# Four-layer cross-attention stack on one Trainium2 core: block transposes of L1's self layers moved behind the next unit's maxima, their DMAs on two queues, V's bias on TensorE, sums of x on ScalarE

## The chip, the core and the metric

The kernel runs on one core of one Trainium2 chip. A core has five engines with queues of their own: TensorE (PE in the profile; PEld is its weight load), VectorE (DVE), ScalarE (ACT), GpSimd (POOL) and SyncE (SP), which here only issues DMAs. All DMAs of the core are carried out by its 16 DMA engines. The metric is the device time of one execution in microseconds.

## The reference

Four layers follow one another on x (4 batches, 1024 tokens, 256 channels) and a context of 77 tokens. L0 is self attention with a mask, cross attention and a feed-forward; L2 and L3 are cross attentions with 16 heads. The change touches L1, which applies its layer three times: the first time to the context, then twice to itself (`enc` attends to `enc`). Cut to what matters:

```python
def _mha_layer(q, k, v, Wq, bq, Wk, bk, Wv, bv, gamma, beta):   # H = 4 heads of 64
    Q = relu(q @ Wq + bq);  K = relu(k @ Wk + bk);  V = relu(v @ Wv + bv)
    scores = einsum('hbqd,hbkd->hbqk', Qh, Kh) / sqrt(64)
    key_mask = sign(abs(sum(k, axis=-1)))
    scores = where(key_mask[None, :, None, :] == 0.0, NEG, scores)
    attn = softmax(scores)
    query_mask = sign(abs(sum(q, axis=-1)))
    attn = attn * query_mask[None, :, :, None]
    out = einsum('hbqk,hbkd->hbqd', attn, Vh) ... + q
    return layer_norm(out, gamma, beta)

q, k, v = queries, keys, values
for i in range(3):
    enc = _mha_layer(q, k, v, Wq[i], bq[i], Wk[i], bk[i], Wv[i], bv[i], gamma[i], beta[i])
    enc = leaky_relu(enc @ Wff[i] + bff[i], negative_slope=0.2) + enc
    q, k, v = enc, enc, enc
```

Everything is computed in fp32. The sum of x over its channels, which gives the two masks, is one of the things that move.

## The kernel before

x stays on the chip, one tile of 128 partitions x 8 x 256 for each batch. The program is a list of items, one for each layer and batch: `Cross16` (L0's cross attention, L2, L3), `Cross4` (L1's first layer, on the context) and `Self4` (L1's layers 1 and 2 on themselves). `Pipe.run` takes them one after the other. An item's attention is cut into units. For `Self4` a unit is a pair of heads p (0 or 1) and a tile t of 128 queries (0 to 7), so an item has 16 units; `Pipe.unit` does one:

1. what was put off as "full" to this unit,
2. `scores(p, t)` (L1206): eight matmul passes into two PSUM tiles `ss`, one for each head (L1213); for each head the maximum over 1024 keys on VectorE, negated (L1224), and the exponential with its sum on ScalarE into `PR` (L1230),
3. what was put off as "next",
4. the pump, which fills in steps of the next item's start (turning x, V, Q and K) and of the last item's end (normalizing, the layer with `Wff`), by their costs,
5. what was put off as "turn", "late" and "col".

`pipe.later(kind, delay, f)` puts a piece of work off to a unit that lies `delay` ahead. The order of TensorE's instructions is the order in which the program writes them. On the other engines the planner of the tile framework sets the order, with buffers and dependencies as it sees them; each engine then runs its queue strictly in order.

The products with V need the exponentials with keys on the partitions. In the branch that the inputs take (`net.blocks`), this is done in blocks of 32: VectorE transposes each 32 x 32 block of `PR` in place (`turned_by_blocks`, L1242), and for each pair of units 16 DMAs of 128 KB (L1249) carry block row a to partition group c of the tile `PT`. All 16 go out on SP's queue. `weighted` (L1285) then multiplies `PT` with V in two halves of eight keys blocks' worth of matmuls, `normal` (L1303 to L1315) turns the result back, divides by the sums and adds x. There are two `PR` buffers, each for a pair of units, two `PT` buffers, and four small PSUM tiles (`p1`) for everything beside the scores.

Three other places matter. `Self4.start` computes the sum of x over channels (L1103) on VectorE, and from it the factor `f` of the query mask and the row `neg` of the key mask; `masks` (L1127) turns `neg` into a row. `values` (L1142) makes V for two tiles of tokens: eight matmul passes, an add of the bias row `brow`, spread over the partitions by a POOL DMA (L1145), and a relu times `f` on ScalarE (L1147). `Layer4.load` fetches a layer's weights and rows; `Net.thirds` (L1992) splits an fp32 row into three bf16 rows, so that a matmul with a row of ones (`ones_rowb`) can add it in PSUM; the layer with `Wff` does that for its bias already (L1353).

Of the kernel before, what the change touches and what calls it, by code (L numbers as in the profile page):

```python
# [9 lines left out]
F32 = mybir.dt.float32  # L10
# [7 lines left out]
P = 128  # L18
# [958 lines left out]
class Layer4:  # L977
# [6 lines left out]
    def load(self):  # L984
# [26 lines left out]
        rows = net.tile("OT", [1, C], name="rows")  # L1011
        nc.sync.dma_start(out=rows, in_=t["rows"][ROW[name] : ROW[name] + 1, C : 2 * C])
        self.rows = net.thirds(rows, C)
        self.brow = net.wpool.tile([P, C], F32, tag="row", name="row", bufs=2)
        nc.gpsimd.dma_start(out=self.brow, in_=t["rows"][ROW[name], 0:C].partition_broadcast(P))
# [67 lines left out]
class Self4(Item):  # L1083
# [4 lines left out]
    def start(self):  # L1088
# [5 lines left out]
        def new():  # L1094
            self.hT = net.tile("C", [P, NC, S], name="hT")
            if l.n:
                self.later_half = False
                self.v = net.tile("D", [P, NT, C], name="V")
            self.nm = net.small.tile([P, NT, 4], F32, tag="nm", name="nm", bufs=2)
            self.sums = net.small.tile([P, NT, 4], F32, tag="sums", name="sums", bufs=2)  # L1100

            sx = net.small.tile([P, NT], F32, tag="sx", name="sx", bufs=2)
            nc.vector.tensor_reduce(sx, x, AX.X, ALU.add)  # L1103
            self.f = net.small.tile([P, NT], F32, tag="f", name="f", bufs=2)
            nc.vector.tensor_scalar(self.f, sx, 0.0, None, ALU.not_equal)
            if l.n:
                self.neg = net.small.tile([P, NT], F32, tag="neg", name="neg", bufs=2)
                nc.vector.tensor_scalar(self.neg, sx, 0.0, MASKED, ALU.is_equal, ALU.mult)
            else:
                self.qt = net.tile("A", [P, 2, S], name="QT")  # L1110
                self.v, self.less = l.v[:, b, :], l.less[:, b : b + 1]
                self.ka = net.work.tile([P, 2, 2, SC], F32, tag="KA", name="KA4", bufs=2)
                nc.gpsimd.memset(self.ka, 0.0)
                for h in range(2):
                    rows = slice(64 * h, 64 * h + 64)
                    nc.gpsimd.tensor_copy(self.ka[rows, :, h, :], l.kt[rows, :, ts(b, SC)])

# [6 lines left out]
        def masks():  # L1124

            pm = net.p1.tile([P, 512], F32, tag="p1", name="pm")
# [11 lines left out]
        def values(t):  # L1138
            pv = net.p1.tile([P, 2, C], F32, tag="p1", name="pv")
            for i in range(2):  # L1140
                for cc in range(NC):
                    nc.tensor.matmul(  # L1142
                        pv[:, i, :], self.hT[:, cc, ts(t + i, P)], l.w["wv"][:, cc, :], start=cc == 0, stop=cc == NC - 1
                    )
            nc.vector.tensor_tensor(pv, pv, l.brow.unsqueeze(1).to_broadcast([P, 2, C]), ALU.add)  # L1145
            for i in range(2):
                nc.scalar.activation(self.v[:, t + i, :], pv[:, i, :], AF.Relu, scale=self.f[:, t + i : t + i + 1])  # L1147

        step(0, new)
        for c in range(2):  # L1150
            step(0.5, turn, c, 0)
            step(0.5, turn, c, 1, lag=2 * c)
# [53 lines left out]
    def scores(self, p, t):  # L1206
# [24 lines left out]
        if net.blocks:  # L1231
            net.pipe.later("turn", 0, lambda: self.turned_by_blocks(p, t, self.pr))
# [3 lines left out]
    def turned_by_blocks(self, p, t, pr):  # L1236
# [10 lines left out]
        for c in range(4):  # L1247
            for a in range(4):
                nc.sync.dma_start(  # L1249
# [4 lines left out]
        for half in range(2):  # L1254
            net.pipe.later("next", 3 + half, lambda half=half: self.weighted(p, t, pt, half, state))
# [179 lines left out]
class Net:  # L1435
# [556 lines left out]
    def thirds(self, row, n):  # L1992

        nc = self.nc
        out = self.work.tile([3, n], BF16, tag="thirds", name="thirds", bufs=2)
# [142 lines left out]
```

## Time and profile before

| | us |
|---|---|
| median of 3 runs (lowest, highest) | 2431.14 (2427.19, 2433.52) |
| the profiled execution | 2428.16 |
| its span | 2426.3 |

| share of the span | busy us | instructions |
|---|---|---|
| PE | 2201.2 (91%) | 11003 |
| DVE | 1620.2 (67%) | 3200 |
| ACT | 907.2 (37%) | 1700 |
| POOL | 104.2 (4%) | 142 |

Times are microseconds from the start of the span. A line of a group names the source line, the engine, the operation, the tile written and the tiles read, the shapes and the number of instructions; behind the bar stand busy time and mean nanoseconds of one, and then how long the engine had stood idle just before them and what ended most of that. A busy time is the time in which at least one instruction of the group ran. The ends of matmuls are modelled, so that a busy PE is not a PE at its peak. A line of the waits names who waited for whom, the sum in us, how often, and the longest. A line of the timeline begins with the start and the length in us. Issues of DMAs are not counted as busy time.

The self layers of L1 fill the stretch from 937 us (first maximum) to 1904 us (last block transpose). In the 100 us from 1400 to 1500, for example, PE is busy for 94.25, DVE for 87.96 and ACT for 45.61, and the DMA engines move 149 GB/s.

### The profile page before, as it was taken

Reading aid. Unit: us, or ns where it says so; the run is one execution under the profiler, and the core shown is the slowest. Engines: PE = TensorE matmul, PEld = TensorE weight load, DVE = VectorE, ACT = ScalarE, POOL = GpSimd, SP = SyncE. Lnnn points to the kernel's source line nnn. Section 1 sums busy time; section 2 is a strip of 40 time slices with the busy share of each in tenths; the row PEclk is TensorE's granted clock in tenths of the full one; section 3 lists DMA queues with packets and bytes.
Section 4 is the critical chain, followed back from the end, with each engine's and each line's share of the span. In section 5 each row is a group of like instructions: output and inputs, shape, how many; then the busy total and the mean of one; then the engine's idle time right before and its main releaser. Section 6 shows DMA issues by size and latency. Waiting matters only on the chain. (4 is left out here: it accounts for less than half of the span.)

```text
span 2426.3 us, 29759 instructions
## 1 busy us (share of the span) xinstructions
PE 2201.2 (91%) x11003; PEld 1233.3 (51%) x11003; DVE 1620.2 (67%) x3200; ACT 907.2 (37%) x1700; POOL 104.2 (4%) x142
## 2 busy tenths in 40 slices
PE   4899999999999989999998999999998898899886
PEld 2566546666768655544444544444444444454332
DVE  5566655444243777888888788888888655565665
ACT  1222342222331544444444445444433343334333
POOL 2000000000000000000000000000000000000000
PEclk7999999999989989999999999989999898899888
DMA  4000010000000001766665666666675300000000
GB/s 127 18 1 16 5 35 1 1 7 5 7 5 3 1 5 45 157 150 139 139 144 134 146 148 148 139 139 139 156 160 130 70 5 1 5 1 1 27 18 28
DMA packets 197593, 158.18 MB, mean 65 GB/s; under 512 B 51327, under 2 KB 196030, under 8 KB 197438
## 3 DMA queue, kind: packets, MB, share of 16 engines
q1 hardware_dynamic: 195374, 152.45, 27.3%
q0 software_dynamic: 1008, 2.68, 0.5%
q8 instruction: 90, 1.47, 0.3%
q10 hardware_dynamic: 1056, 1.05, 0.1%
q14 instruction: 65, 0.53, 0.1%
HBM read 17.67 MB, written 4.19 MB: 9 GB/s over the span
## 5 line engine op out<-in xcount | busy, mean ns | idle before, releaser
L1230 ACT ACTIVATE PR<-ss,nm 128x1024 f32<-128x1024 f32 x256 | 284.4, 1113 | 398.9 <-DVE nm L1224 313.1
L1242 DVE STREAM_TRANSPOSE PR<-PR 128x2048 f32<-128x2048 f32 x128 | 295.8, 2311 | 113.4 <-ACT PR L1230 109.9
L1213 PE MATMUL ss<-QK 64*128 64x512 f32 x1024 | 336.9, 650 | 38.1 <-ACT PR L1230 37.8
L1224 DVE TENSOR_REDUCE nm<-ss 128x1 f32<-128x1024 f32 x256 | 299.8, 1210 | 9.5 <-PE ss L1213 9.4
L1285 PE MATMUL po<-PT,V 128*64 128x256 f32 x2048 | 261.3, 399 | 9.0 <-DMA PT<-PR 6.8
L356 ACT ACTIVATE PT<-pb 77x1024 f32<-77x1024 f32 x192 | 185.4, 1016 | 173.7 <-PE pb L352 173.7
L1285 PEld LDWEIGHTS po<-PT,V 128*64 128x64 f32 x2048 | 141.7, 141 | 171.6 <-issue 109.2
L1213 PEld LDWEIGHTS ss<-QK 64*128 64x128 f32 x1024 | 116.7, 193 | 181.9 <-ACT PR L1230 105.7
L275 DVE TENSOR_REDUCE mx<-pa 128x4 f32<-128x308 f32 x384 | 157.6, 469 | 74.2 <-PE pa L270 73.1
L270 PE MATMUL pa<-KA,QT 64*128 64x308 f32 x768 | 170.9, 499 | 33.7 <-DVE mx L275 31.1
L270 PEld LDWEIGHTS pa<-KA,QT 64*128 64x128 f32 x768 | 103.4, 201 | 101.9 <-DVE mx L275 46.8
L365 PE MATMUL po<-PT,Vc 77*32 77x512 f32 x768 | 135.7, 646 | 18.9 <-ACT PT L356 10.2
L1452 ACT COPY OT<-po 128x512 f32<-128x512 f32 x57 | 33.4, 586 | 230.1 <-PE po L365 218.4
L595 PE MATMUL pp<-w,hid 128*128 128x256 f32 x512 | 114.0, 381 | 0.0
L580 PE MATMUL pp<-hF,w 128*128 128x256 f32 x512 | 113.2, 379 | 0.0
L346 PE MATMUL pb<-QT,KA 32*77 32x512 f32 x768 | 112.7, 658 | 0.0
L595 PEld LDWEIGHTS pp<-w,hid 128*128 128x128 f32 x512 | 96.5, 190 | 15.9 <-DVE mx L275 2.5
L580 PEld LDWEIGHTS pp<-hF,w 128*128 128x128 f32 x512 | 97.1, 190 | 14.6 <-issue 1.3
L1483 DVE BATCH_NORM_STATS2 st<-x 128x6 f32<-128x256 f32 x256 | 97.9, 404 | 5.6 <-DMA x<-in_x 4.4
L1356 PE MATMUL pp<-wo,hE 128*128 128x256 f32 x384 | 96.4, 393 | 1.6 <-ACT hE L1459 1.5
L588 ACT ACTIVATE hid<-pp,cols 128x256 f32<-128x256 f32 x64 | 30.4, 474 | 175.7 <-PE pp L580 175.7
L260 PE MATMUL pp<-hT,wq 128*128 128x512 f32 x192 | 91.2, 611 | 1.8 <-DVE hT L1450 1.0
(253 smaller groups left out, 3042.3 us busy)
## 6 DMA issues: line engine op xcount, KB each, us to landing
PT<-PR SPq DMA_DIRECT2D x1024, 128.0 KB
x<-in_x SPq DMA_DIRECT2D x4, 1024.0 KB
out<-x SPq DMA_DIRECT2D x8, 512.0 KB
w<-in_ff_w SPq DMA_DIRECT2D x2, 1024.0 KB
gb<-in_norms POOLq DMA_DIRECT2D x5, 256.0 KB, 4.8
wk<-in_l_wk SPq DMA_DIRECT2D x10, 128.0 KB
wv<-in_l_wv SPq DMA_DIRECT2D x5, 256.0 KB
wq<-in_l_wq SPq DMA_DIRECT2D x10, 128.0 KB
```

The costliest lines, as they stand in the source:

```text
L270: nc.tensor.matmul(pas[i], self.qt[rows, e, ts(t, P)], self.ka[rows, e, :, :], start=True, stop=True)
L275: nc.vector.tensor_reduce(out, pas[i].rearrange("p (j s) k -> p j s k", s=2), AX.X, ALU.max, negate=True)
L346: nc.tensor.matmul(pbs[j // 2][:SC, j % 2, :], self.ka[rows, e, 2 * (j % 2) + s, :], self.qt[rows, e, ts(c, 512)], start=True, stop=False,)
L356: nc.scalar.activation(pt[:, 2 * i : 2 * i + 2, :], pbs[i][:SC], AF.Exp, scale=self.l.scale)
L365: nc.tensor.matmul(po[ts(j, h.slot), :], l.v[:, self.b, col : col + h.vw], pt[:, j, :], start=True, stop=True)
L580: nc.tensor.matmul(pp[:, i, :], self.w1[:, cc, ts(f + i, P)], s["hT"][:, cc, ts(q, 2 * P)], start=cc == 0, stop=cc == NC - 1)
L595: nc.tensor.matmul(pp[:, u, :], s["a"][:, f, ts(u, P)], self.w2[:, f, :], start=f == 0, stop=f == NF - 1)
L1213: nc.tensor.matmul(ss[h][:, k, :], self.qk[p][rows, 0, ts(t, P)], self.qk[p][rows, 1, ts(k, 512)], start=True, stop=True,)
L1224: nc.vector.tensor_reduce(self.nm[:, t, at], s2, AX.X, ALU.max, negate=True)
L1230: nc.scalar.activation(out, s2, AF.Exp, bias=self.nm[:, t, at], accum_out=self.sums[:, t, at])
L1242: nc.vector.transpose(part, part)
L1285: nc.tensor.matmul(po[64 * h : 64 * h + 64], self.v[:, k, 64 * (2 * p + h) : 64 * (2 * p + h) + 64], pts[:, :, h, :, k, :] if net.blocks e ...
```

## The change

- The block transpose of a unit (with the 16 DMAs after each second one) is put off to "next" of the following unit, which is behind that unit's maxima in the program; before it stood at "turn" of its own unit.
- Of the 16 DMAs, those with odd a go out on POOL's queue and those with even a on SP's.
- The products with V are put off to "turn", 2 and 3 units after the transpose's new place; that is the same unit as before, but behind the pump's steps instead of ahead of them.
- The bias of V is added in PSUM by a matmul with a row of ones and the three thirds of the bias (`vrows`), in layers 1 and 2; the add on VectorE and the POOL DMA of the bias row go. `load` makes a second set of thirds, and `thirds` gets four buffers instead of two.
- The sum of x over channels comes from ScalarE in layers 1 and 2: an activation for each tile of tokens that writes a copy nobody reads and accumulates the sum, two of them after each turning step; the masks are made from it in `masks`.

```diff
@@ Layer4.load
-        rows = net.tile("OT", [1, C], name="rows")
-        nc.sync.dma_start(out=rows, in_=t["rows"][ROW[name] : ROW[name] + 1, C : 2 * C])
-        self.rows = net.thirds(rows, C)
-        self.brow = net.wpool.tile([P, C], F32, tag="row", name="row", bufs=2)
-        nc.gpsimd.dma_start(out=self.brow, in_=t["rows"][ROW[name], 0:C].partition_broadcast(P))
+        def thirds(at):
+            rows = net.tile("OT", [1, C], name="rows")
+            nc.sync.dma_start(out=rows, in_=t["rows"][ROW[name] : ROW[name] + 1, at : at + C])
+            return net.thirds(rows, C)
+
+        self.rows = thirds(C)
+        if self.n:
+            self.vrows = thirds(0)
+        else:
+            self.brow = net.wpool.tile([P, C], F32, tag="row", name="row", bufs=2)
+            nc.gpsimd.dma_start(out=self.brow, in_=t["rows"][ROW[name], 0:C].partition_broadcast(P))
@@ Self4.start
-            sx = net.small.tile([P, NT], F32, tag="sx", name="sx", bufs=2)
-            nc.vector.tensor_reduce(sx, x, AX.X, ALU.add)
-            self.f = net.small.tile([P, NT], F32, tag="f", name="f", bufs=2)
-            nc.vector.tensor_scalar(self.f, sx, 0.0, None, ALU.not_equal)
-            if l.n:
-                self.neg = net.small.tile([P, NT], F32, tag="neg", name="neg", bufs=2)
-                nc.vector.tensor_scalar(self.neg, sx, 0.0, MASKED, ALU.is_equal, ALU.mult)
-            else:
+            self.sx = net.small.tile([P, NT], F32, tag="sx", name="sx", bufs=2)
+            if not l.n:
+                nc.vector.tensor_reduce(self.sx, x, AX.X, ALU.add)
+                marks()
...
+        def marks():
...
+        def sums(t):
+            out = net.tile("F", [P, 2, C], name="xs")
+            for i in range(2):
+                nc.scalar.activation(out[:, i, :], x[:, t + i, :], AF.Identity, accum_out=self.sx[:, t + i : t + i + 1])
@@ masks
+            marks()
@@ values
+            nc.tensor.matmul(pv, net.ones_rowb, l.vrows.unsqueeze(1).to_broadcast([3, 2, C]), start=True, stop=False)
...
-            nc.vector.tensor_tensor(pv, pv, l.brow.unsqueeze(1).to_broadcast([P, 2, C]), ALU.add)
@@ the steps of start
         for c in range(2):
-            step(0.5, turn, c, 0)
-            step(0.5, turn, c, 1, lag=2 * c)
+            for cc in range(2):
+                step(0.5, turn, c, cc, lag=2 * c * cc)
+                if l.n:
+                    step(0, sums, 4 * c + 2 * cc)
@@ scores
-            net.pipe.later("turn", 0, lambda: self.turned_by_blocks(p, t, self.pr))
+            net.pipe.later("next", 1, lambda pr=self.pr: self.turned_by_blocks(p, t, pr))
@@ turned_by_blocks
-                nc.sync.dma_start(
+                (nc.sync, nc.gpsimd)[a % 2].dma_start(
...
-            net.pipe.later("next", 3 + half, lambda half=half: self.weighted(p, t, pt, half, state))
+            net.pipe.later("turn", 2 + half, lambda half=half: self.weighted(p, t, pt, half, state))
@@ Net.thirds
-        out = self.work.tile([3, n], BF16, tag="thirds", name="thirds", bufs=2)
+        out = self.work.tile([3, n], BF16, tag="thirds", name="thirds", bufs=4)
```

More of the change, by code (lines that the diff above doesn't have):

```diff
@@ L1116, in new @@
                     nc.gpsimd.tensor_copy(self.ka[rows, :, h, :], l.kt[rows, :, ts(b, SC)])
+        def marks():
+            self.f = net.small.tile([P, NT], F32, tag="f", name="f", bufs=2)
+            nc.vector.tensor_scalar(self.f, self.sx, 0.0, None, ALU.not_equal)
+            if l.n:
+                self.neg = net.small.tile([P, NT], F32, tag="neg", name="neg", bufs=2)
+                nc.vector.tensor_scalar(self.neg, self.sx, 0.0, MASKED, ALU.is_equal, ALU.mult)
+        def sums(t):
+            out = net.tile("F", [P, 2, C], name="xs")
+            for i in range(2):
+                nc.scalar.activation(out[:, i, :], x[:, t + i, :], AF.Identity, accum_out=self.sx[:, t + i : t + i + 1])
         def turn(c, cc):
@@ L1142, in values @@
                     nc.tensor.matmul(
-                        pv[:, i, :], self.hT[:, cc, ts(t + i, P)], l.w["wv"][:, cc, :], start=cc == 0, stop=cc == NC - 1
+                        pv[:, i, :], self.hT[:, cc, ts(t + i, P)], l.w["wv"][:, cc, :], start=False, stop=i + cc == NC
                     )
-            nc.vector.tensor_tensor(pv, pv, l.brow.unsqueeze(1).to_broadcast([P, 2, C]), ALU.add)
             for i in range(2):
@@ L1150, in start @@
         for c in range(2):
-            step(0.5, turn, c, 0)
-            step(0.5, turn, c, 1, lag=2 * c)
+            for cc in range(2):
+                step(0.5, turn, c, cc, lag=2 * c * cc)
+                if l.n:
+                    step(0, sums, 4 * c + 2 * cc)
         if l.n:
```

## The prediction

> **What bounds the kernel now.** I read the page's slices first, to find the stage that the change touches, then its groups, then the waits, the timeline and tables of windows inside that stage, and last the DMA traffic. The slices and groups of the page:
>
> ```profile
> DVE  5566655444243777888888788888888655565665
> ...
> DMA  4000010000000001766665666666675300000000
> ...
> L1230 ACT ACTIVATE PR<-ss,nm 128x1024 f32<-128x1024 f32 x256 | 284.4, 1113 | 398.9 <-DVE nm L1224 313.1
> L1242 DVE STREAM_TRANSPOSE PR<-PR 128x2048 f32<-128x2048 f32 x128 | 295.8, 2311 | 113.4 <-ACT PR L1230 109.9
> ...
> L1224 DVE TENSOR_REDUCE nm<-ss 128x1 f32<-128x1024 f32 x256 | 299.8, 1210 | 9.5 <-PE ss L1213 9.4
> ```
>
> The slices with DMA at 5 to 7 are the two self layers of L1: 128 units (2 layers, 4 batches, 16 units each). They run from 937 to 1904 us, 7.56 us a unit. There ScalarE waits for the maxima (313.1 us), and VectorE's only large wait is that of the block transpose for the exponentials (109.9 us). Units 64 to 79 (batch 0 of layer 2) are a stretch without layer loads; their waits and a table of windows, in which the last columns are granted clock, DMA share and GB/s:
>
> ```profile
> ACT PR L1230 <- DVE nm L1224: 35.6, 11, 4.5
> ...
> DVE PR L1242 <- ACT PR L1230: 14.4, 12, 1.3
> ACT V L1147 <- DVE pv L1145: 12.6, 4, 3.8
> ```
>
> ```profile
> 1416.50:1533.10 116.60, 108.60 (x531) 53.05 (x527) 100.61 (x124) 54.11 (x104) 2.71 (x3) 0.99 0.64 147
> 1200.00:1209.00 9.00, 8.93 (x53) 5.50 (x49) 7.61 (x14) 3.14 (x6) 0.00 (x0) 1.00 0.88 203
> 971.50:973.50 2.00, 2.00 (x18) 1.06 (x16) 2.00 (x3) 0.00 (x0) 0.00 (x0) 1.00 1.01 178
> 973.50:974.50 1.00, 1.00 (x10) 0.86 (x8) 0.97 (x4) 0.12 (x1) 0.00 (x0) 1.00 1.04 320
> 974.50:978.50 4.00, 3.44 (x15) 2.26 (x15) 2.73 (x3) 3.72 (x9) 0.00 (x0) 1.00 1.13 202
> ```
>
> Of 116.6 us VectorE is busy for 100.6; the 16.0 left are nearly all its wait for ScalarE. So VectorE's queue sets the pace: unit time is its work plus that wait. One unit in the timeline:
>
> ```profile
> 1222.01 0.67 DVE L1145 TENSOR_TENSOR pv<-pv,row 128x512 f32<-128x512 f32 x1
> 1222.59 2.34 DVE L1224 TENSOR_REDUCE nm<-ss 128x1 f32<-128x1024 f32 x2
> ...
> 1223.83 1.11 ACT L1230 ACTIVATE PR<-ss,nm 128x1024 f32<-128x1024 f32 x1 [0.28 <-DVE nm L1224]
> ...
> 1224.96 1.11 ACT L1230 ACTIVATE PR<-ss,nm 128x1024 f32<-128x1024 f32 x1
> 1225.08 3.11 PE L1213 MATMUL ss<-QK 64*128 64x512 f32 x8 [0.39 <-ACT PR L1230]
> ...
> 1226.19 2.31 DVE L1242 STREAM_TRANSPOSE PR<-PR 128x2048 f32<-128x2048 f32 x1 [1.27 <-ACT PR L1230]
> ```
>
> Maxima, exponentials, and then VectorE stands 1.27 us until the second exponential is written; only then come the transpose and what is queued behind it.
>
> **The change, part by part.** The five clean batches (1, 2, 4, 5, 6) take 119.4, 118.2, 116.6, 119.9 and 115.3 us from first maximum to first maximum: mean 117.9, or 7.37 a unit. All savings are counted against 7.37; times are against the profiled run (2428.2 us, span 2426.3), which lies 3 below the median 2431.1.
>
> *Transpose behind the next unit's maxima.* The transpose now finds its exponentials long written; the wait (110 us) goes. VectorE's work stays.
>
> *Bias of V on TensorE.* Four adds a batch of 0.68 us leave VectorE (2.7 us), four ones-row matmuls of 0.32 from start to start (the same form at L1353) come to TensorE: 1.3 us. ScalarE's wait for the add (81.5 us in 28) goes too; it was covered.
>
> *Sums of x on ScalarE.* One reduction of 2.28 us a batch leaves VectorE. ScalarE gets 8 activations of at most 0.47 (V's row, 128x256) and 8 accumulator reads of 0.19: 5.3 us a batch on an engine busy 54 of 117. It costs nothing while it does not stand before an exponential; without that cover up to 0.66 for each.
>
> *Floors after these three.* VectorE: 100.6 - 2.7 - 2.3 = 95.6 a batch, 5.97 a unit. TensorE: a unit's scores (1.99) and products with V (1.95) are 63 a batch; 4 V's (1.99), 4 forwards (about 2.3 with the ones row), 8 projections (1.98, half with a ones row) about 35, 48 transposes of 0.11, and 1.3 new: 105 at most; merged rows contain 0.2 of overlapping tail, so about 101, 6.3 a unit, and 6.6 at the stage's granted clock of about 0.95. The loop scores, maximum, exponential, exponential is 2.24 + 0.14 + 1.98 + 1.2 = 5.6. So without the DMAs a unit would take about 6.6.
>
> *What is late next: the block DMAs.* A pair of units (2k, 2k+1) fills one of two PR buffers; 16 DMAs of 128 KB empty it; the first exponential of unit 2k+4 may write it again only when all have landed. So far they start after the transpose in unit 2k+1. Call D the time from the end of that transpose to the last landing. In the trace the 16th issue ends 10.4 to 11.8 us after it, the last packet 11.8 to 13.4, and the exponential comes at 14.6 to 18.5: it was free. Now the transpose of unit 2k+1 comes after the maxima of unit 2k+2, about 1.17 + 2.31 us past the moment at which that unit's first exponential could run, plus 0.4 for what stands between in a few units: 3.9. Follow the loop over four units: exponential of 2k+2, two rounds of the loop (L each) to the maximum of 2k+4, 3.9, then D, then the exponential of 2k+6, which uses the same buffer. So a unit takes the larger of 6.6 and (2L + 3.9 + D)/4. The products with V are due later in unit 2k+4 than before (behind the other matmuls), so they are not the first to wait.
>
> *D with two queues.* SP issues one block DMA each 0.648 us; with eight on SP and eight on POOL, whose issues take 0.53 to 0.60 us, issue ends at about 5 us. Then the transfers set D: first packet 1.3 us after the issue, 2.1 MB at some rate, and 0.35 for the semaphore (landing of POOL's small loads against their last packet). The rate is in the windows above. SP alone moves 203 GB/s with the DMA engines 88% busy. When a POOL load (gb, issued at 970.29) had blocked the blocks, the backlog first ran at 320 GB/s for 1 us, then for 4 us at 202, with the share up to 1.13: more in flight, hardly more moved. In that stretch, by the packet records of the trace, the packets' lag behind their issues fell from 2.58 to 2.00 us over 8 DMAs, which is 0.596 us each, 220 GB/s. Bounds: 178 GB/s (the window in which both queues moved) gives D = 1.65 + 11.8 = 13.4; 320 gives 8.2. I take 215, near the long backlog: D = 1.65 + 9.8 = 11.4.
>
> The Trainium skill (DMA: Bandwidth & Descriptors, section "Issuing engines are not separate DMA queues") says that issuing from several engines saves only the sequencers' issue time, because all run on the same 16 DMA engines. By that rule the rate stays at 203, D is 12.0 and the sum below about 19 us higher; the window at 202 agrees with it, the one at 320 doesn't.
>
> *Sum.* L lies between 5.6 and 6.6; I take 6.4. (12.8 + 3.9 + 11.4)/4 = 7.03 a unit: 0.34 saved x 128 = 43 us.
>
> *POOL's queue.* Each norm's power (L1336, 1.07 us) now shares a queue with the DMAs: behind eight issues it waits 5 us, with two units of slack before its reader in the built order. Bounds 0 to 1 us for each of 16; I take 0.
>
> *Second row of thirds.* Layers 1 and 2 each cast and load one more row: three casts of 0.27, two subtractions of 0.40 and four DMAs on SP between block DMAs. In layer 2 the present load made batch 3 last 127.8, 10 more than the clean mean; one pair's issues stretched to 19.8 us. Bounds 0 and +10; I take +6, as half the blocks now avoid SP. Layer 1's load meets no block DMAs.
>
> Total: -43 + 6 = -37, so 2428.2 - 37 = about 2391 us.
>
> **The rivals.**
> - *The blocks bind nobody.* The two queues drift apart and the drain is nearer 320 GB/s; D is below 9.7 and the unit falls to 6.6: -99 + 6, 2335 us (2320 to 2355). For: the 320 window. Against: it held for 1 us.
> - *No gain.* 203 GB/s and a loop of 6.6: (13.2 + 3.9 + 12.0)/4 = 7.28, -12 + 6: 2422, up to 2435. For: the 202 window.
> - *Slower: two queues in each other's way.* Place: the DMA engines while SP and POOL blocks are both queued. At 178 GB/s D is 13.4 and, with L up to 6.6, the unit 7.63; with POOL's later first packet (1.75 after issue) 7.75: +33 to +49, plus 6 to 10: 2470 to 2485. It decides from D = 12.4 (about 195 GB/s) on. For: the 178 window, where SP's packets nearly stopped. Against: that load read HBM, the blocks don't.
> - *Slower: VectorE holds up POOL's issues.* If each of the eight waits for the end of a VectorE instruction (1.2 us mean), issue takes 9.6 and D is 1.65 + 9.6 + 1.2 = 12.5 at least, and, with more than one instruction each, 14: 2435 to 2490. Against: POOL's loads in this stage went in 0.60 us beside a busy VectorE and their first packets followed in 1.3 to 1.8.
>
> The Trainium skill (SBUF — State Buffer, box "The 'DVE blocks DMA' trap") has a rule of this last kind: DMAs issued from GpSimd wait for descriptors while VectorE runs a two-port copy. No long VectorE copy runs in this stage.
>
> **How the numbers follow.** Forecast 0.45 (7.25 to 6.75 a unit: 2355 to 2419), blocks bind nobody 0.18, no gain 0.10, queues collide 0.18, VectorE holds POOL 0.09. A measurement of this kernel tells 0.3% (7.3 us) from no change, so faster 0.63, same 0.09, slower 0.28. The range 2330 to 2450 leaves out half of the slower cases and a little of the fast one; the forecast's own is 2355 to 2419.
>
> **What would show it.** The transpose's wait for ScalarE near 0; no V add and no sums on VectorE; the first exponential of even units waiting for the DMA of PT in the list of waits; last landings about 11 us behind the transpose. I am wrong if that wait is absent and the unit is near 6.6, or if DMA rates with both queues are under 195 GB/s.

## The result and the profile after

The changed kernel takes 2422.7 us (median of 7 runs, 2417.5 to 2426.6) against 2432.9 for the kernel before on the same chip: ratio 0.9954, interval 0.9941 to 0.9968. That is 10 us less, where the prediction had 37 less. The profiled run took 2419.1 us, span 2417.3. Lines below the change have moved: scores L1230, maxima L1241, exponentials L1247, transpose L1259, block DMAs L1266, products with V L1302.

The page of the changed kernel, VectorE's slices and the costliest groups (busy, mean ns of one, idle before):

```profile
DVE  5566655444233666888889688878887655655665
...
L1247 ACT ACTIVATE PR<-ss,nm 128x1024 f32<-128x1024 f32 x256 | 284.8, 1114 | 381.1 <-DVE nm L1241 294.4
L1259 DVE STREAM_TRANSPOSE PR<-PR 128x2048 f32<-128x2048 f32 x128 | 295.8, 2311 | 130.4 <-ACT PR L1247 115.5
L1266 POOL DMA_DIRECT2D PT<-PR x512 | 279.8, 554 | 591.9 <-PE ss L1230 227.9
...
L1241 DVE TENSOR_REDUCE nm<-ss 128x1 f32<-128x1024 f32 x256 | 299.7, 1210 | 20.0 <-PE ss L1230 19.9
```

The transposes' wait for ScalarE, which was to go, is still there: 109.9 us before, 115.5 now. Half of the blocks are on POOL, as written. Units 64 to 79 by windows (us, then busy time of PE, PEld, DVE, ACT, POOL, granted clock, DMA share, GB/s) and by waits (us, times, longest):

```profile
1409.98:1524.35 114.37, 109.68 (x545) 54.65 (x544) 96.52 (x125) 56.95 (x120) 37.59 (x68) 1.00 0.71 152
```

```profile
DVE PR L1259 <- ACT PR L1247: 15.3, 12, 1.7
...
ACT xs L1130 <- DVE x L1380: 11.9, 4, 3.3
```

VectorE's work fell from 100.6 to 96.5 us, but the batch only from 116.6 to 114.4: of the 4.1 us taken off VectorE, 1.9 came back as idle time. One unit (89) in the timeline shows why the wait stayed:

```profile
1589.88 2.34 DVE L1241 TENSOR_REDUCE nm<-ss 128x1 f32<-128x1024 f32 x2
...
1591.13 1.11 ACT L1247 ACTIVATE PR<-ss,nm 128x1024 f32<-128x1024 f32 x1 [3.81 <-DVE nm L1241]
...
1592.26 1.12 ACT L1247 ACTIVATE PR<-ss,nm 128x1024 f32<-128x1024 f32 x1
...
1593.50 2.31 DVE L1259 STREAM_TRANSPOSE PR<-PR 128x2048 f32<-128x2048 f32 x1 [1.27 <-ACT PR L1247]
...
1597.03 1.22 DVE L1241 TENSOR_REDUCE nm<-ss 128x1 f32<-128x1024 f32 x1
```

After two maxima VectorE again stands 1.27 us, transposes the same unit's block, and only then comes the next maximum (1597.03). The program's text puts the transpose behind the next unit's maxima; the planner, which orders VectorE's queue, put it ahead of them, in the same place as before.

The two self layers (first maximum to last transpose; busy time and granted clock from one window each, the waits summed over VectorE's instructions in the trace, short ones included; the page counts waits above 0.15 us alone). Kernels other than the first two are those of the next section. "Half" is the time in the stage at a granted clock of 0.50, from the trace's clock records.

| kernel | median us | ratio (95%) | stage us | VectorE busy | idle | transpose for ScalarE | clock | half, us |
|---|---|---|---|---|---|---|---|---|
| before | 2432.9 | | 966.6 | 814 | 152 | 109.9 | 0.96 | 75 |
| changed | 2422.7 | 0.9954 (0.9941-0.9968) | 950.3 | 787 | 164 | 115.6 | 0.98 | 47 |
| transposes_own | 2420.2 | 0.9948 (0.9935-0.9961) | 950.4 | 787 | 164 | 114.1 | 0.97 | 50 |
| products_own | 2412.7 | 0.9909 (0.9887-0.9932) | 940.2 | 786 | 155 | 105.6 | 0.98 | 41 |
| own_place | 2398.7 | 0.9868 (0.9849-0.9887) | 934.0 | 785 | 149 | 103.9 | 0.99 | 27 |
| queues_alone | 2397.3 | 0.9865 (0.9841-0.9890) | 931.4 | 809 | 123 | 89.7 | 0.99 | 27 |
| sums_alone | 2414.9 | 0.9926 (0.9905-0.9946) | 952.8 | 802 | 151 | 115.3 | 0.97 | 51 |
| bias_alone | 2435.6 | 1.0010 (0.9994-1.0027) | 963.9 | 799 | 165 | 112.2 | 0.97 | 58 |
| own_brow | 2389.8 | 0.9821 (0.9807-0.9834) | 926.0 | 799 | 127 | 95.2 | 0.99 | 17 |
| deferred | 2440.1 | 1.0030 (1.0019-1.0041) | 970.5 | 790 | 181 | 0 | 0.96 | 84 |
| one_queue | 2493.4 | 1.0257 (1.0232-1.0283) | 1026.2 | 789 | 238 | 153.7 | 0.95 | 99 |
| split | 2332.7 | 0.9583 (0.9566-0.9600) | 869.0 | 811 | 57 | 16.2 | 1.00 | 7 |

### The profile page after: what moved, and what is told of

It reads as the page before. It is cut to its first block, busy times and chain, and to the rows that moved or that the text cites. A ratio compares the mean times of both kernels' runs of the same rounds, so it can differ in the third digit from the quotient of the medians.

```text
span 2417.3 us, 31250 instructions
## 1 busy us (share of the span) xinstructions
PE 2196.4 (91%) x11035; PEld 1226.0 (51%) x11035; DVE 1582.1 (65%) x3170; ACT 928.9 (38%) x1828; POOL 382.3 (16%) x652
## 3 DMA queue, kind: packets, MB, share of 16 engines
q0 software_dynamic: 25488, 69.56, 12.8%
## 5 line engine op out<-in xcount | busy, mean ns | idle before, releaser
L1247 ACT ACTIVATE PR<-ss,nm 128x1024 f32<-128x1024 f32 x256 | 284.8, 1114 | 381.1 <-DVE nm L1241 294.4
L1259 DVE STREAM_TRANSPOSE PR<-PR 128x2048 f32<-128x2048 f32 x128 | 295.8, 2311 | 130.4 <-ACT PR L1247 115.5
L1266 POOL DMA_DIRECT2D PT<-PR x512 | 279.8, 554 | 591.9 <-PE ss L1230 227.9
L1230 PE MATMUL ss<-QK 64*128 64x512 f32 x1024 | 322.9, 630 | 26.3 <-ACT PR L1247 26.1
L1241 DVE TENSOR_REDUCE nm<-ss 128x1 f32<-128x1024 f32 x256 | 299.7, 1210 | 20.0 <-PE ss L1230 19.9
L1302 PE MATMUL po<-PT,V 128*64 128x256 f32 x2048 | 252.4, 389 | 2.3 <-DVE mx L275 2.2
L1230 PEld LDWEIGHTS ss<-QK 64*128 64x128 f32 x1024 | 112.7, 188 | 172.0 <-ACT PR L1247 94.5
L1302 PEld LDWEIGHTS po<-PT,V 128*64 128x64 f32 x2048 | 137.1, 138 | 106.1 <-issue 46.3
L1509 POOL TENSOR_TENSOR pw<-va,minus_half 128x4 f32<-128x4 f32 (+1 forms) x28 | 38.0, 1358 | 619.7 <-DVE va L1507 542.0
L595 PEld LDWEIGHTS pp<-w,hid 128*128 128x128 f32 x512 | 96.5, 190 | 15.9 <-DVE mx L275 2.5
```

Of the source, the lines that this page charges most:

```text
L595: nc.tensor.matmul(pp[:, u, :], s["a"][:, f, ts(u, P)], self.w2[:, f, :], start=f == 0, stop=f == NF - 1)
L1230: nc.tensor.matmul(ss[h][:, k, :], self.qk[p][rows, 0, ts(t, P)], self.qk[p][rows, 1, ts(k, 512)], start=True, stop=True,)
L1241: nc.vector.tensor_reduce(self.nm[:, t, at], s2, AX.X, ALU.max, negate=True)
L1247: nc.scalar.activation(out, s2, AF.Exp, bias=self.nm[:, t, at], accum_out=self.sums[:, t, at])
L1259: nc.vector.transpose(part, part)
L1266: (nc.sync, nc.gpsimd)[a % 2].dma_start(out=pt[ts(c, 32), :, :, a].rearrange("p t h k j -> p (t h) (k j)"), in_=pr[ts(a, 32), :, :, ts(c, ...
```

## The experiments

**Deferred in fact, and the second queue.** The first four kernels test the prediction's main line. `issue_after` tells the planner to keep an instruction behind a given one; with it the transpose truly stands behind the next unit's maxima.

`deferred`, the changed kernel with

```diff
-            nc.vector.tensor_reduce(self.nm[:, t, at], s2, AX.X, ALU.max, negate=True)
+            net.last = nc.vector.tensor_reduce(self.nm[:, t, at], s2, AX.X, ALU.max, negate=True)
...
-        nc.vector.transpose(part, part)
+        with net.tc.issue_after(net.last.ins):
+            nc.vector.transpose(part, part)
```

> The changed kernel with an issue-order edge: each block transpose is queued on VectorE behind the second maximum of the following unit. Theory: in the changed kernel the planner put every transpose back behind its own unit's exponentials, so the wait for ScalarE stayed (115.6 us in 88 times); held behind the next maxima it falls below 15 us, and a unit falls from 7.43 us to about 7.0 (the loop formula of the prediction with D near 11.5), 40 to 60 us less than the changed kernel, ratio to the kernel before 0.972 to 0.98. Rival: TensorE or the landing of the blocks takes the wait's place at once; the wait for ScalarE goes, but exponentials wait for the DMA of PT or scores for TensorE, and the ratio stays at 0.99 to 1.00.

`deferred_sp`, the same with all 16 DMAs on SP's queue:

```diff
-                (nc.sync, nc.gpsimd)[a % 2].dma_start(
+                nc.sync.dma_start(
```

> As the run with the held transposes, but all 16 block DMAs on SP's queue. If the landing of the blocks binds once the transposes are late, as the formula (2L + 3.9 + D)/4 has it, D rises from about 11.5 to 12.5 us and the time by 30 us or so against that run (ratio about 0.985 to 0.99). If the blocks bind nobody, the two runs agree within 0.2%.

`own_place`, the changed kernel with transposes and products put back in the program, all else kept:

```diff
-            net.pipe.later("next", 1, lambda pr=self.pr: self.turned_by_blocks(p, t, pr))
+            net.pipe.later("turn", 0, lambda: self.turned_by_blocks(p, t, self.pr))
...
-            net.pipe.later("turn", 2 + half, lambda half=half: self.weighted(p, t, pt, half, state))
+            net.pipe.later("next", 3 + half, lambda half=half: self.weighted(p, t, pt, half, state))
```

> The changed kernel with the transposes and the products with V put back to their old places in the program (turn 0, next 3 and 4); two queues, V's bias on TensorE and sums on ScalarE stay. Theory: VectorE's order hardly depends on that place, so the time is that of the changed kernel, ratio to before 0.995 within 0.003, and the transpose waits for ScalarE as long. Rival: placing the products with V behind the pump's steps is what gave the gain; then this run is at 1.000 or above.

`one_queue`, the changed kernel with the edit of `deferred_sp` alone:

> The changed kernel with all 16 block DMAs on SP's queue. Theory: since the transposes stayed in their own unit, the first exponential of each second unit comes 15 to 18 us after the transpose and the blocks have landed by 12 to 13, so the second queue gains nothing: ratio to before 0.995 within 0.002. Rival: the second queue is worth something at the layer loads, where SP's issues stretched to 19.8 us: 3 to 8 us slower than the changed kernel, ratio 0.997 to 0.999.

Measured: deferred 2440.1 (1.0030), deferred_sp 2521.1 (1.0381, 1.0358 to 1.0405), own_place 2398.7 (0.9868), one_queue 2493.4 (1.0257). None came out as expected: deferred is above both of its forecasts, own_place below both, and deferred_sp lies 81 us above deferred, where the loop formula gave 30. The page of deferred:

```profile
L1247 ACT ACTIVATE PR<-ss,nm 128x1024 f32<-128x1024 f32 x256 | 284.5, 1114 | 332.4 <-DVE nm L1241 261.8
...
L1241 DVE TENSOR_REDUCE nm<-ss 128x1 f32<-128x1024 f32 x256 | 301.1, 1217 | 73.9 <-PE ss L1230 73.7
L1303 PE MATMUL po<-PT,V 128*64 128x256 f32 x2048 | 272.4, 412 | 54.8 <-DMA PT<-PR 36.9
...
L1260 DVE STREAM_TRANSPOSE PR<-PR 128x2048 f32<-128x2048 f32 x128 | 294.6, 2302 | 0.0
```

Here the wait is gone (0.0), and the time is longer than before. It came back as maxima waiting for scores (73.7), as VectorE's normalization waiting for TensorE's turned output (62.4 us in 21), and as TensorE waiting for blocks at the products with V (36.9). Unit 92 of deferred in the timeline:

```profile
1632.81 2.36 DVE L1241 TENSOR_REDUCE nm<-ss 128x1 f32<-128x1024 f32 x2
...
1635.08 2.30 DVE L1260 STREAM_TRANSPOSE PR<-PR 128x2048 f32<-128x2048 f32 x1
...
1638.32 1.11 ACT L1247 ACTIVATE PR<-ss,nm 128x1024 f32<-128x1024 f32 x1 [1.35 <-DMA PT<-PR]
...
1638.46 1.95 PE L1303 MATMUL po<-PT,V 128*64 128x256 f32 x16 [2.23 <-DMA PT<-PR]
...
1641.04 0.70 DVE L1331 TENSOR_TENSOR pt<-pt,r 128x512 f32<-128x512 f32 x1 [3.65 <-PE pt L1321]
```

Transposes run straight behind the maxima, but the blocks of an earlier pair land only between 1637 and 1638: the exponential and the products wait for them, and VectorE then waits 3.65 us for the transposes that stand behind those products in TensorE's queue. In batch 5 the three units with such a wait took 9.1 to 10.1 us, ten of the other 13 took 5.3 to 6.9, the last three 7.6 to 9.1. From the end of the transpose to the last packet the blocks take 11.7 us (median of 64 pairs); the prediction's 11.4, less its 0.35 for the semaphore, is 11.05.

The 19 exponentials that waited for blocks started 0.6 to 1.4 us after the last packet and not 0.35, that is 12.2 to 13.5 us behind the transpose (median 12.8). With D = 12.8 the prediction's own formula, (12.8 + 3.9 + 12.8)/4, gives 7.38 us a unit, no saving against its 7.37; the five clean batches of deferred took 7.41. That is an estimate, and the agreement may be luck, since only 19 of 62 such exponentials waited and the products with V were a second waiter that the prediction had ruled out. deferred_sp does not fit the formula: its last packet is only 0.3 us later (12.0).

one_queue showed that the second queue is worth 71 us in the changed kernel (2493.4 against 2422.7), of which the rival had expected 3 to 8: there the last packet comes only 0.5 us later than with two (12.1 and 11.6 us behind the transpose, medians). Its timeline shows another effect, ScalarE's queue:

```profile
1545.32 0.42 ACT L1130 ACTIVATE xs<-x 128x256 f32<-128x256 f32 x1 [1.57 <-DVE x L1380]
...
1546.13 1.09 ACT L1247 ACTIVATE PR<-ss,nm 128x1024 f32<-128x1024 f32 x1
...
1547.37 4.43 PE L1230 MATMUL ss<-QK 64*128 64x512 f32 x8 [2.44 <-ACT PR L1247]
...
1548.44 2.31 DVE L1259 STREAM_TRANSPOSE PR<-PR 128x2048 f32<-128x2048 f32 x1 [3.22 <-DMA PT<-PR]
```

Both maxima were ready at 1543.9, but two sums of x stand ahead of the exponential and wait for the residual add; exponential, scores and transpose are late behind them. (The transpose's wait is put down to a DMA; it also started 0.1 us after the second exponential ended.) The planner gives each variant another order, so this is no price of the queue alone.

**The parts one at a time.** `queues_alone`, `bias_alone` and `sums_alone` are the kernel before with one part of the change each; `own_no_sums` is own_place with the sums back on VectorE. The core of each:

```diff
 queues_alone
-                nc.sync.dma_start(
+                (nc.sync, nc.gpsimd)[a % 2].dma_start(
 bias_alone
+            nc.tensor.matmul(pv, net.ones_rowb, l.vrows.unsqueeze(1).to_broadcast([3, 2, C]), start=True, stop=False)
-            nc.vector.tensor_tensor(pv, pv, l.brow.unsqueeze(1).to_broadcast([P, 2, C]), ALU.add)
 sums_alone
-            nc.vector.tensor_reduce(sx, x, AX.X, ALU.add)
+                if l.n:
+                    step(0, sums, 4 * c + 2 * cc)
```

> The kernel before with the block DMAs split over SyncE's and GpSimd's queues, nothing else. Theory A (a queue of issues held the kernel before in places: 16 issues of 0.65 us are 10.4 us, and one_queue lost 2.6%): the median falls by 1 to 1.5%, ratio 0.985 to 0.990, and VectorE's 3.5 us of transposes waiting for the DMA of PT stay small. Theory B (the DMAs were free before, by the 1.2 us and more between the last packet and the next exponential): ratio 0.998 to 1.002.

> The kernel before with V's bias in the matmul, nothing else. Theory A (VectorE's queue is the bound in this stage, its work counts in full): 4 adds of 0.68 us a batch are 2.7 us, 8 batches 21.6 us, ratio about 0.991, less up to 6 us for the second row of thirds. Theory B (work taken from VectorE comes back as its wait for ScalarE's exponentials): within 0.997 to 1.002, with the wait of the transposes for ScalarE (109.9 us before) up by some 15 to 20 us.

> The kernel before with the sums of x on ScalarE, nothing else. Theory A (the sums stand before exponentials in ScalarE's queue and wait there for the residual add): one reduction of 2.28 us a batch leaves VectorE, 8 times 0.66 us and the waits for x come before exponentials; net ratio 1.003 to 1.012, and xs waiting for x of about 50 us in the list of waits. Theory B (VectorE's work counts, the sums are covered): 8 x 2.28 = 18 us less, ratio 0.9925.

> own_place (2398.7 us) with the sums of x back on VectorE as in the kernel before: the bias and the two queues are left of the change. Theory A (the sums on ScalarE cost more than they bring): below 2395, ratio 0.975 to 0.984. Theory B (they bring their 2.28 us a batch): about 2398.7 + 18 = 2417, ratio 0.993.

Measured: queues_alone 2397.3 (0.9865), bias_alone 2435.6 (1.0010), sums_alone 2414.9 (0.9926) and own_no_sums 2411.8 (0.9922, 0.9899 to 0.9946). The queue gives 35 us, as Theory A had it, and by far the most. The sums give 18, as Theory B had it. The bias gives nothing: VectorE has 15.5 us less to do in the stage and 12.9 more to wait (table), though not where Theory B had it (the transposes' wait for ScalarE rose by 2.3 us, the maxima's for scores from 9.4 to 16.3), and the first maximum comes 6.5 us later (943.5 against 937.0). Next to the two queues the bias even costs: own_no_sums against queues_alone is 14.5 us slower, in the traces 10 ahead of the stage (first maximum at 944.0 against 934.0), 9.4 in it and 4.9 won back behind it. Batch 3, which loads layer 2, is 9.8 longer (125.3 against 115.5).

Where the queue's 35 us come from: 12.3 of the stage's 35.2 lie in batch 3 (127.8 to 115.5). The kernel before there, in the timeline:

```profile
1328.54 0.57 SPq L2001 DMA_DIRECT2D thirds<-third  x1
1329.15 0.60 SPq L1249 DMA_DIRECT2D PT<-PR  x1
...
1330.60 0.57 SPq L2001 DMA_DIRECT2D thirds<-third  x1
...
1331.21 14.23 SPq L1249 DMA_DIRECT2D PT<-PR  x20
...
1340.79 1.11 ACT L1230 ACTIVATE PR<-ss,nm 128x1024 f32<-128x1024 f32 x1 [7.69 <-DMA PT<-PR]
...
1340.82 3.48 PE L1285 MATMUL po<-PT,V 128*64 128x256 f32 x16 [4.79 <-DMA PT<-PR]
```

SP's queue runs in order: each `thirds` DMA waits for a cast on VectorE, and block DMAs stand behind it, one between two of them; the pair's other 12 go only from 1331.2 on (the row of 20 runs into the next pair), and ScalarE stands 7.69 us and TensorE 4.79. With half of the blocks on POOL this jam is gone. The other 23 us are spread over the batches, 0.8 to 7.0 in each. There the landing is 0.5 us earlier (medians 12.1 and 11.6), the planner's order differs, and the time at half clock falls from 75 to 27 us; what share belongs to which was not separated.

The bias's cost in batch 3, in own_place's timeline:

```profile
1324.65 0.60 PE L1155 MATMUL pv<-thirds,ones_rowb 3*128 3x512 bf16 x1 [3.16 <-DMA thirds<-third]
...
1329.00 0.84 ACT L1162 ACTIVATE V<-pv,f 128x256 f32<-128x256 f32 x2 [7.99 <-PE pv L1158]
...
1335.43 2.36 DVE L1241 TENSOR_REDUCE nm<-ss 128x1 f32<-128x1024 f32 x2 [8.82 <-PE ss L1230]
```

The ones-row matmul needs the second row of thirds, the last thing that the load brings; TensorE stands at it, all of V's products follow, and the next scores come so late that VectorE is idle for 8.82 us.

**The two moves, and a cut that does what the deferral was for.** `own_brow` is own_place without the bias (queues and sums only). `products_own` and `transposes_own` are the changed kernel with one of the two moves taken back. `split` is own_brow with each transpose in two halves, one for each head: the first half needs only the first exponential, so it can fill the 1.27 us in which VectorE stands.

```diff
 products_own
-            net.pipe.later("turn", 2 + half, lambda half=half: self.weighted(p, t, pt, half, state))
+            net.pipe.later("next", 2 + half, lambda half=half: self.weighted(p, t, pt, half, state))
 transposes_own
-            net.pipe.later("next", 1, lambda pr=self.pr: self.turned_by_blocks(p, t, pr))
+            net.pipe.later("turn", 0, lambda pr=self.pr: self.turned_by_blocks(p, t, pr))
-            net.pipe.later("turn", 2 + half, lambda half=half: self.weighted(p, t, pt, half, state))
+            net.pipe.later("turn", 3 + half, lambda half=half: self.weighted(p, t, pt, half, state))
 split
-        part = pr[:, t % 2].rearrange("p h s -> p (h s)")
-        nc.vector.transpose(part, part)
+        for h in range(2):
+            part = pr[:, t % 2, h]
+            nc.vector.transpose(part, part)
```

> The kernel before with two queues and the sums of x on ScalarE; V's bias and the moves are undone. Theory A (the parts add: queues_alone -35 us, sums_alone -18 us): about 2380 us, ratio 0.978, batch 3 (the load of layer 2) near 116 us and not 126. Theory B (the planner's order decides, not the parts): as own_place and queues_alone, 2397 to 2400, ratio 0.986.

> The changed kernel with the products with V issued ahead of the unit's other work again (same unit as in the kernel before); transposes stay behind the next unit's scores in the program's text. Theory A (the moved transposes cost what own_place gained back): about 2420, ratio 0.995. Theory B (the moved products cost it): about 2399, ratio 0.986.

> The changed kernel with the block transposes issued in their own unit again; the products with V stay behind the unit's other work. Theory A (the moved transposes cost it): about 2399, ratio 0.986. Theory B (the moved products cost it): about 2420, ratio 0.995.

> own_brow with each block transpose cut into two halves, one for each head, so that the first half can run while ScalarE writes the second head's exponentials. Theory A (VectorE's queue with its 1.27 us wait for the second exponential sets the unit; the wait can be taken away without moving a transpose behind the next unit's maxima): the bare unit falls from 5.87 to 4.8 to 5.0, until TensorE's 6.3 to 6.6 binds; some 80 us below own_brow, ratio 0.945 to 0.955. Theory B (the wait only covers for others: blocks, scores or products bind right behind it): less than 25 us below own_brow, the wait coming back as maxima waiting for scores or as transposes waiting for the DMA of PT.

Measured: own_brow 2389.8 (0.9821), between its two theories: the queue and the sums add up to 53 us and gave 44. transposes_own 2420.2 against 2422.7 for the changed kernel, with overlapping intervals, the same stage (950.4 and 950.3) and the same VectorE work and waits (table): where the program writes the transpose made no difference next to the moved products. products_own 2412.7: putting the products back gives 10 us, but its six runs fall into two groups, 2406 to 2408 and 2418 to 2421, and the trace is of the upper one. Both moves taken back (own_place) give 24. So moving the products costs 10 us beside moved transposes and 21 beside unmoved ones, and moving the transposes 2 or 14; neither theory has it all. Those 14 are not explained: TensorE's queue in products_own is that of own_place as far as the traces have its records, the queues of VectorE, ScalarE and POOL differ only around 948 to 985 and 1306 to 1321 us, and of the 18.8 us between the two traces only 6.2 lie in the stage; 8.4 lie ahead of it (first maximum at 946.1 against 937.7), where all queues are the same, and 4.1 behind it.

What the moved products do can be seen in units 107 and 108 of the changed kernel, which took 6.3 and 9.7 us where own_place took 5.9 and 7.3:

```profile
1723.79 0.58 ACT L1476 COPY hE<-pt 128x512 f32<-128x512 f32 x1
...
1723.94 1.31 PE L1230 MATMUL ss<-QK 64*128 64x512 f32 x2 [1.58 <-ACT PR L1247]
1724.25 1.13 ACT L1247 ACTIVATE PR<-ss,nm 128x1024 f32<-128x1024 f32 x1
...
1725.52 3.78 PE L1230 MATMUL ss<-QK 64*128 64x512 f32 x6 [0.27 <-ACT PR L1247]
...
1730.38 0.59 ACT L1476 COPY hE<-pt 128x512 f32<-128x512 f32 x1 [4.54 <-PE pt L1364]
...
1731.07 1.11 ACT L1247 ACTIVATE PR<-ss,nm 128x1024 f32<-128x1024 f32 x1
...
1733.40 2.31 DVE L1259 STREAM_TRANSPOSE PR<-PR 128x2048 f32<-128x2048 f32 x1 [2.06 <-ACT PR L1247]
```

A copy has slipped between two exponentials; TensorE waits 1.58 us, then runs six matmuls of the scores in 3.78 us at a clock of 0.50; the next copy, ahead of unit 108's exponentials in ScalarE's queue, waits 4.54 us for it, and exponentials and transpose are late by that. It is one place; the sum was not taken apart further.

split is the fastest kernel of the study: 2332.7 us, 0.9583 of the kernel before and 57 us below own_brow, between its theories (80 and 25 us). Its page and a unit of it:

```profile
L1258 DVE STREAM_TRANSPOSE PR<-PR 128x1024 f32<-128x1024 f32 x256 | 305.6, 1225 | 16.8 <-ACT PR L1245 7.0
L1239 DVE TENSOR_REDUCE nm<-ss 128x1 f32<-128x1024 f32 x256 | 300.8, 1216 | 11.9 <-PE ss L1228 10.7
```

```profile
1617.62 2.35 DVE L1239 TENSOR_REDUCE nm<-ss 128x1 f32<-128x1024 f32 x2
...
1620.02 1.11 ACT L1245 ACTIVATE PR<-ss,nm 128x1024 f32<-128x1024 f32 x1
...
1620.34 2.37 DVE L1258 STREAM_TRANSPOSE PR<-PR 128x1024 f32<-128x1024 f32 x2
```

The transposes start while the second exponential runs; two halves take 2.37 us, the whole took 2.31. VectorE's idle time in the stage falls from 127 to 57 us. What may bind next is in the window of units 64 to 79:

```profile
1360.05:1467.68 107.63, 104.91 (x539) 54.04 (x539) 100.17 (x143) 58.06 (x120) 37.27 (x67) 1.00 0.75 162
```

TensorE is busy for 104.9 of 107.6 us at full clock: 6.7 us a unit, near the prediction's floor of 6.6. That TensorE binds is a reading and was not tested alone: its busy time is no fixed amount of work, since about the same matmuls were busy for 883.3 us in own_brow's stage and 846.1 in split's. Waits for blocks do not bind it: the first exponential into a PR buffer starts at least 1.7 us after the last packet of the blocks that leave it.

**What was still open.** `bias_one_load` is own_place with both bias rows cast and loaded as one row of 512 (and `thirds` back at two buffers); `split_one_load` puts the same on top of split; `split_after` is the changed kernel with the cut transposes alone; `deferred_late` is deferred with the products one unit later; `split_before` is the kernel before with the cut alone.

```diff
 bias_one_load
+        rows = net.tile("OT", [1, 2 * C], name="rows")
+        nc.sync.dma_start(out=rows, in_=t["rows"][ROW[name] : ROW[name] + 1, 0 : 2 * C])
+        both = net.thirds(rows, 2 * C)
+        self.rows = both[:, C : 2 * C]
...
+            self.vrows = both[:, 0:C]
 deferred_late
-            net.pipe.later("turn", 2 + half, lambda half=half: self.weighted(p, t, pt, half, state))
+            net.pipe.later("turn", 3 + half, lambda half=half: self.weighted(p, t, pt, half, state))
```

> own_place with both rows of a layer's biases cast and loaded together as one row of 512 (three casts and three DMAs instead of six and six, in the same order). Theory A (the second row's own chain of casts and DMAs costs own_place some 8 us ahead of the first self layer and 10 in batch 3): batch 3 near 116 us, first maximum near 935, median 2380 to 2385, ratio 0.978 to 0.981. Theory B (the ones-row matmuls and the order on TensorE cost it): 2394 to 2400, ratio 0.985.

> split with V's bias on TensorE too, both rows loaded as one, so that all of the change but the moves stands beside the cut transposes. Theory A (VectorE's queue still sets most units): 8 x 2.7 = 21 us below split at most, 2315 to 2325, ratio 0.951 to 0.955. Theory B (TensorE has become the bound and gets 32 matmuls of 0.385 us more): 2333 to 2345, ratio 0.959 to 0.963.

> The changed kernel with each block transpose cut into two halves, one for each head, nothing else. Theory A (the transposes' wait for ScalarE is still there in the changed kernel, 115.6 us, and is what the change left standing): 80 to 100 us below it, 2322 to 2343, ratio 0.955 to 0.963. Theory B (the changed kernel is held by the loads and the products, the wait is cover): 2385 to 2410, ratio 0.980 to 0.990.

> deferred (2440.1 us) with the products with V one unit later still. Theory A (with truly late transposes the products were the first to wait for the blocks; one unit more covers the landing): the waits of TensorE at the products for the DMA of PT go, the median falls to 2385 to 2405, ratio 0.980 to 0.989. Theory B (the two buffers of PT or of PR bind next): the wait moves to the exponentials or to the block DMAs' issue, 2425 or more, ratio 0.997 or more.

> The kernel before with nothing but the block transposes cut into two halves, one for each head. Theory A (the cut is worth the same 57 us with one queue as it was from own_brow to split): about 2376 us, ratio 0.977. Theory B (with SyncE's queue alone the blocks and loads bind as soon as units are shorter, 16 issues of 0.65 us and the landing being 11.8 to 13.4 us of two units): 2395 to 2415, ratio 0.984 to 0.993.

Measured:

| kernel | median us | ratio (95%) | reading |
|---|---|---|---|
| bias_one_load | 2391.8 | 0.9838 (0.9816-0.9860) | 7 us below own_place, with overlapping intervals; what the stage gains in the trace is all in batch 3 (126.1 to 119.4), and the first maximum hardly moves (937.7 to 937.0). Half of Theory A |
| split_one_load | 2335.5 | 0.9608 (0.9586-0.9630) | the time of Theory B, VectorE's 2.7 us a batch are worth nothing; but the stage is 3.3 us shorter than split's and the first maximum 5.8 later, so that its reason is not shown |
| split_after | 2351.5 | 0.9665 (0.9646-0.9684) | 71 us below the changed kernel, short of Theory A's 80: the wait that the change left standing was worth it |
| deferred_late | 2458.9 | 1.0121 (1.0095-1.0147) | Theory B, see below |
| split_before | 2396.2 | 0.9858 (0.9841-0.9875) | the time of Theory B: the cut gives 35 us with one queue, 57 with two queues and the sums. That blocks bind is not shown: only in batch 3 does an exponential wait for them |

The page of deferred_late:

```profile
L1241 DVE TENSOR_REDUCE nm<-ss 128x1 f32<-128x1024 f32 x256 | 301.6, 1218 | 139.0 <-PE ss L1230 138.9
...
L1260 DVE STREAM_TRANSPOSE PR<-PR 128x2048 f32<-128x2048 f32 x128 | 294.6, 2302 | 0.0
L1303 PE MATMUL po<-PT,V 128*64 128x256 f32 x2048 | 254.9, 392 | 5.6 <-ACT hT L1477 4.4
```

The products no longer wait for blocks (36.9 us in deferred, 0.9 here), but the exponentials do: 54.7 us in 22, against 34.2 in 19. Maxima wait 138.9 us for scores. So with late transposes something waited for the landing at both places of the products: the products, or the exponentials that need the PR buffer back.

## Why the prediction was right or wrong

*Which engine sets the pace.* Right in the main. split, which takes only VectorE's wait away and adds a little work to VectorE, gains 57 us, and its unit of 6.7 us is near the floor given for TensorE. But VectorE's work does not count in full: bias_alone took 15.5 us off it in the stage, and the stage got 2.7 shorter.

*"The transpose now finds its exponentials long written; the wait (110 us) goes."* This is the step that failed. On the chip the wait is 115.5 us, since the planner sets VectorE's order and put the transpose in its old place; the built queues show no deferral at all, and taking the move back in the program (transposes_own) changed the time by 2.5 us, inside the intervals. The prediction counted -43 us for the transposes and the blocks behind them, more than its whole -37. The step read the program's order as the queue's order; in VectorE's built queue a transpose follows each two maxima in both kernels, and the first follows two maxima and not four.

*"Not the first to wait."* Had the deferral happened, the forecast would still have failed. deferred measures it: 2440 and not 2391. D came out at 12.8 us where exponentials waited, not 11.4: the last packet landed 0.65 later than counted, and the exponential came some 1.0 after it and not 0.35. Issue did not end at about 5 us: POOL's eight did at 5.0, SP's only at 8.1. Neither of the two slower rivals shows here: POOL's issues took 0.55 us each, and 2.1 MB in 10.4 us (11.7 less the 1.3 to the first packet) are about 202 GB/s, an estimate that is below the 215 taken and above the 195 named. And besides the exponentials the products with V waited (36.9 us), in front of everything else that TensorE had to do.

*The second queue.* Priced only as what makes a later transpose bearable; by itself it was held to bind nobody. It is the largest part: -35 us alone. The jam behind `thirds` was in the trace of before, and the prediction used it only as a price for the second row. The Trainium skill (DMA: Bandwidth & Descriptors, section "Issuing engines are not separate DMA queues") says that a second issuing engine saves only issue time, usually little. The landing agrees in kind: issue ends 8.0 us behind the transpose instead of 10.5, landing improves by 0.5. But the 12.3 us of batch 3 show that what stands behind a waiting issue has to be counted too, and the rule doesn't; how the other 23 come about is open.

*The bias.* -2.7 us of VectorE a batch was the work, not the time: alone it gave +2.4 us (interval -1.5 to +6.6, from the ratio). The second row of thirds, forecast at +6 with "Layer 1's load meets no block DMAs", costs 8 to 10 in batch 3 (bias_alone 136.0 against 127.8) and about 6 ahead of the first unit: the first maximum comes at 936.7 us in the mean of the six traces with one row of thirds (934.0 to 939.6), at 942.3 in the mean of the eleven with two (937.7 to 946.1). Traces with the same queues up to there differ by up to 8.4 us, so that a single pair says little. ScalarE's wait for a buffer that the thirds' parts hold grows there from 5.1 us before to 8.9 in bias_alone and 7.6 in own_place; whether that is the cause is not settled.

*The sums.* -2.3 us a batch, 18 in all: sums_alone gave 18. That they could stand before an exponential was said, and one_queue shows it, but beside the kernel before's order it cost nothing that can be seen.

*The moves in the program.* Counted at nothing for the products; together they cost 24 us (own_place against the changed kernel), by a way that one place shows and the sum leaves open.

So the terms, part by part from the kernel before over queues_alone, own_no_sums and own_place to the changed kernel, are: queue -35, bias +14, sums -13, the two moves +24. As steps of one chain they must add up to the -10 measured; that they do is no test of them, and in another order they have other sizes (bias alone +2, sums alone -18). The direction was right by luck, by parts which the forecast did not count on. The median lies at the 2422 of the rival "no gain", also by luck and not by its mechanism. The list of waits puts 29.2 us in 9 waits of exponentials down to blocks (35.9 in 11 before), but those nine began 0.08 us after their maximum and at least 5.1 us after the last packet: in the changed kernel no exponential waited for blocks.

## What to carry to other kernels

Where a planner orders a queue, look for the moved instruction in the built queue before pricing the move; a later line in the program may move nothing. A wait for the second of two producers may be better filled by cutting the consumer in two than by putting it off: here the cut gave 35 to 71 us in three kernels, the deferral a loss. And count for each in-order queue what stands behind an instruction that waits, small loads on a DMA queue and copies ahead of exponentials included.

## What the runs showed of the hardware

TensorE's clock falls in steps. It is either 1.00 or 0.50, in pieces of 3.41 us, and in the stage of the kernel before each of the 12 falls followed a piece in which TensorE was busy for 0.19 to 0.63 of the time (though not each such piece led to a fall). The kernel before around unit 91, by windows:

```profile
1614.70:1616.60 1.90, 1.90 (x19) 1.08 (x17) 1.86 (x4) 0.00 (x0) 0.00 (x0) 1.00 0.89 204
1618.50:1622.00 3.50, 3.49 (x8) 1.11 (x8) 2.40 (x2) 1.93 (x5) 0.00 (x0) 0.78 0.44 100
1622.50:1626.00 3.50, 3.50 (x17) 1.72 (x16) 2.88 (x7) 2.30 (x4) 0.00 (x0) 0.50 0.70 160
```

The fall at 1620.45 followed a wait of only 1.26 us, which ended at 1618.5; the 16 products that took 1.95 us at 1614.7 take 3.68 at 1622.5. The Trainium skill (TensorE: Matmul & The Clock Gate, section "HAM oscillation — how this bites in real kernels") warns of idle gaps above about 3.4 us; the piece's length agrees, but here a fall followed a gap of a third of it. Over the kernels of the table without the cut and with the transposes in place, a stage is longer the more time it spends at half clock (17 us: 926; 27: 931 and 934; 41: 940; 47 and 50: 950; 51: 953; 58: 964; 75: 967; one_queue, with 99, lies above the row at 1026), though their work on VectorE differs too (785 to 814 us). The falls follow waits, and matmuls at half clock make others wait; which part of a stage's time is due to the clock alone was not tried.

A second issuing queue slowed the first one's issues. In queues_alone, which differs from the kernel before in nothing else, an issue of a block DMA on SP took 0.80 us (median of 512, up to 1.94) against 0.60 before; on POOL it took 0.55. All kernels here with half of the blocks on POOL have SP's issues at 0.76 to 0.86 us, all with one queue at 0.60. So POOL's eight issues end 4.9 us behind the transpose, and SP's eight only at 8.0.
